# The first tile of x in four quarters over two DMA queues, in an attention and LoRA mixture layer

## The chip, the cores and the metric

The kernel runs on one core of a Trainium2 chip. The metric is the device time of one execution in microseconds, the median of several. One further execution is profiled; its page and trace are what this document reads. A core has TensorE (PE: matrix products, with weight loads shown as PEld), VectorE (DVE), ScalarE (ACT), GpSimd (POOL) and SyncE (SP), each with its own instruction queue; they wait for each other on semaphores. SP issues the DMAs that move data between HBM and the on-chip memory SBUF. Products land in PSUM, whose banks have to be copied out by DVE or ACT before they are used again.

## The reference

2048 tokens (4 sequences of 512) of width 1024, all in float32. Normalisation is without weights: subtract the mean, divide by the root of variance plus 1e-5.

```
x = x + layernorm(attention(layernorm(x)))
x = x + layernorm(ffn(layernorm(x)))

attention: qkv = x @ w_qkv.T + b_qkv           # 32 query heads, 8 key/value heads of 32
           rotate q and k (rope); causal softmax(q k.T / sqrt(32)) v; @ w_o.T + b_o
ffn:       logits = x @ gate_w.T; softmax over the best 2 of 8 experts, 0 for the others
           x @ base_w.T + base_b + 2 * sum over experts of weight * (x @ A.T) @ B.T   # rank 16
```

## The kernel before, in words

**Tiling.** The tokens are cut into 16 tiles of 128, one token a partition. A tile goes through: normalising x (`xa`, its statistics in `stats`), transposing it (`pt_xn`, copied out to `T_xn`), keys and values (`acc_kv`, then `raw_k` rotated and transposed as `pt_k`), queries (`acc_q`, `raw_q` rotated, transposed as `pt_q`, copied out to `qT`), attention, output projection (`acc_o`), two normalisations, transposes `pt_h`, gate and LoRA (`acc_gl`, `pt_low`) and the base product (`acc_f`).

**Pairs and mixed weights.** Queries, output projection and base product are computed for pairs of tiles with seven block products instead of eight (function `seven`), on sums and differences of activations (`s_q`, `s_o`, `s_f`) and of weights. The mixed weights are made once: `mix` loads rows, combines them on DVE or POOL (`mix_q`, `mix_o`, `mix_f`) and stores them to HBM. This takes place during the first third of the run. Weights for the products stream in as pieces of 128x512 (`piece`, L489) through a ring of 13.

**Attention.** A group is some heads of one tile: four rows of heads at once. Group t_a is tile t from head block a. Scores go to `sc` (L1446); DVE adds the causal mask (L1515) and takes the maximum (L1525) in two halves; ACT takes exponentials and their sums (L1467); DVE the reciprocal (`rtot`, L1496); POOL scales (`pr`, L1481); TensorE transposes each of the four parts (`pt_p`, L1541: pt_p_t_a_0 to _3), ACT or DVE copies them out (`prT`), and TensorE multiplies by the values (`av`, L1564).

**What sets the order.** The kernel is not scheduled by the framework. A planner inside it (`class Order`) goes through the work with assumed durations when the program is built. Chains of operations are Python generators that yield an `Op` (work for one of DVE, ACT, POOL, SP, with a time for each engine that may take it), a `Task` to wait for, or a delay in microseconds. The loop `tensor` always picks the next step for TensorE among the lanes (scores, transposes, values, dense products) by what the plan says is ready at the planned time; `_next` picks for the other engines. The order in which the planner decides is the order of each engine's instruction queue in the finished program; on the chip, semaphores alone decide when each starts. Every planned time feeds into later decisions, all through the plan.

**The first tile.** `load_x` brings a tile's x in two halves of 128x512 on SP (L870) and `normed_x` follows: statistics for each half as it lands (`Norm.half`, L524), the aggregate (L533), adding 1e-5 (L537), the root and the shift on POOL (L541, L545), scaling of the two halves on DVE or ACT (`Norm.apply`), transposes (L593). In the plan a DMA takes its kilobytes over 370 per microsecond on SP and lands 2.8 us later (`LANDS`). For the first tile (`jobs[0]`) nothing stands before it; after `job.issued` the loads of the key and value weights (`wkv_sb`, eight of 256 KB) follow on SP, then pieces, biases and the rotation table. All later tiles share the one buffer `xa`.

`Norm.quarter` (L502), statistics over 256 columns, is in the kernel already; it is used for the very last tile of tokens. Issued DMAs take eight completion semaphores in turn, so a DMA waits until the eighth before it has landed.

Of the kernel before, what the change touches and what calls it, by code (L numbers as in the profile page):

```python
# [91 lines left out]
class Order:  # L92
# [10 lines left out]
    def start(self, chain, at=0.0):  # L103
        task = Task()
        self._go_on(chain, task, at)
        return task
# [159 lines left out]
def kernel(  # L266
# [14 lines left out]
    nc = tc.nc  # L281
# [4 lines left out]
    NH = D // 512  # L286
# [29 lines left out]
    order = Order(banks)  # L316
    start = order.start

    def dve(us, urgent, issue):
        return Op(urgent, dve=(us, issue))  # L320
# [7 lines left out]
    def sp(us, issue, urgent=0):  # L328
        return Op(urgent, sp=(us, issue))
# [9 lines left out]
    def combine(urgent, out, in0, in1, op, engines=("dve", "pool")):  # L339
# [17 lines left out]
        out=earlier,  # L357
        in_=earlier,
# [17 lines left out]
    LANDS = 2.8  # L376
# [118 lines left out]
    class Norm:  # L495
# [6 lines left out]
        def quarter(self, src, k):  # L502

            if self.stats is None:
                self.stats = small.tile(
                    [P, 2 * NH, 6], F32, tag="stats4", bufs=1, name=f"stats_{self.name}"
                )
            cols = slice(k * 256, (k + 1) * 256)
            yield dve(
                0.4,  # L510
                self.urgent,
                lambda: nc.vector.bn_stats(out=self.stats[:, k, :], in_=src()[:, cols]),
            )
# [68 lines left out]
    def transposes(dst, src, halves, name, slot):  # L582


        steps, ready = [], []
        for h in range(NH):
            ready.append(Task())

            def issue(h=h):
                pt = ps.tile([P, 4, P], F32, tag="ps", name=f"pt_{name}_{h}")  # L590
                for c in range(4):
                    at = (4 * h + c) * P
                    nc.tensor.transpose(pt[:, c, :], src()[:, at : at + P], ident)  # L593

                def end():
                    yield step.done
                    yield copy(512, lambda: dst()[:, 4 * h : 4 * h + 4, :], lambda: pt)
                    banks.give(order.at)
                    ready[h].finish(order.at)

                step = steps_of[h]
                start(end(), order.now)

            steps.append(Step(0.44, issue, [halves[h], slot], bank=True, turns=True))
        steps_of = list(steps)
        return steps, ready
# [238 lines left out]
    jobs = [Job(tok, f"{tok.t}", has_q=tok.t != first) for tok in tokens]  # L845
# [7 lines left out]
    def load_x(job):  # L853

        yield xa_slots.take()
        if job is not jobs[0]:
            yield has_wk

        rows = slice(job.tok.t * P, (job.tok.t + 1) * P)
        job.xn = xpool.tile([P, D], F32, tag="xa", bufs=1, name=f"xa_{job.name}")  # L860

        def lands(h):
            yield LANDS
            job.in_x[h].finish(order.at)

        for h in range(NH):
            cols = slice(h * 512, (h + 1) * 512)
            yield sp(
                P * 512 * 4 / 1024 / RATE,
                lambda: nc.sync.dma_start(out=job.xn[:, cols], in_=x[rows, cols]),  # L870
            )
            start(lands(h), order.at)
        job.issued.finish(order.at)
# [14 lines left out]
    def normed_x(job):  # L888

        norm = Norm(f"1_{job.name}", 3)  # L890
        halves = [Task() for _ in range(NH)]

        def normed():
            for h in range(NH):
                yield job.in_x[h]
                yield from norm.half(lambda: job.xn, h)
            yield from norm.scale()
            for h in range(NH):
                yield from norm.apply(lambda: job.xn, lambda: job.xn, h)
                halves[h].finish(order.at)  # L900

        start(normed())
        taken = Task()

        def take_slot():
            yield halves[0]
            yield xnT_slots.take()
            taken.finish(order.at)

        start(take_slot())  # L910
        turns, job.ready = transposes(job.xnT, lambda: job.xn, halves, f"xn_{job.name}", taken)

        def free_x():
            yield [s.done for s in turns]
            xa_slots.give(order.at)

        start(free_x())
        return turns
# [720 lines left out]
    for job in jobs:  # L1639
        start(load_x(job))  # L1640
# [169 lines left out]
```

## Time and profile before

| | us |
|---|---|
| median of 3 runs | 1167.19 (1167.12 to 1168.61) |
| the profiled execution | 1167.07 |
| its span, first to last instruction | 1165.3 |
| TensorE busy (matmul) | 1139.3, 98% of the span |
| DVE, POOL, ACT busy | 829.1, 601.5, 529.2 |
| granted TensorE clock | 0.999 |
| share of the chain that ended last on TensorE | 90% |

A line of the profile's order of time has the start in us, the duration in us, engine, source line, operation, tile written <- tiles read, shape and count (a count over one merges neighbours). In square brackets stands how long the engine was idle before and what released it. A source line can be a helper's. Buffer numbers are left out of the tile names. A matrix product of 128x512 in float32 shows as two matmul records.

The first transposes of the first tile start at 7.34 us; the last product ends near 1157.8.

### The profile page before, as it was taken

The numbers are of one execution on the slowest core, as the hardware profiler recorded it, in microseconds if no ns is written. First come the engines' busy times: TensorE is split into PE (matmuls) and PEld (weight loads), VectorE is DVE, ScalarE is ACT, GpSimd is POOL, SyncE is SP. The second block draws the span as 40 slices with busy tenths as digits, with TensorE's granted clock in tenths as the row PEclk, the third lists the DMA queues.
The fourth block names the chain that finished last, engine by engine and source line by source line (L and its number), as shares of the span: only waits on it lengthen the run. The fifth ranks groups of instructions, "written<-read, shape, count | busy, mean of one in ns | idle before, by whom it ended". The sixth has DMA issues, their size and how long they took to land.

```text
span 1165.3 us, 21509 instructions
## 1 busy us (share of the span) xinstructions
PE 1139.3 (98%) x7284; PEld 632.8 (54%) x7284; DVE 829.1 (71%) x1635; ACT 529.2 (45%) x1543; POOL 601.5 (52%) x847
## 2 busy tenths in 40 slices
PE   7999999999999999999999999999999999999997
PEld 3555555655556555565555555456555555555455
DVE  4787878887777757688767775768866787668453
ACT  0354555445545355555534355455644555444011
POOL 2686846743756435555545353544645564446221
PEclk9999999999999999999999999999999999999999
DMA  9879778453772637635477443683457744574893
GB/s 346 290 244 316 248 251 286 168 173 104 252 242 80 211 103 248 188 95 165 144 244 253 141 140 109 197 262 102 144 173 230 243 139 160 179 261 144 274 317 117
DMA packets 118317, 232.54 MB, mean 200 GB/s; under 512 B 13504, under 2 KB 14528, under 8 KB 118208
## 3 DMA queue, kind: packets, MB, share of 16 engines
q1 hardware_dynamic: 118208, 231.16, 60.7%
q8 instruction: 59, 0.97, 0.3%
q14 instruction: 50, 0.41, 0.1%
HBM read 210.14 MB, written 20.97 MB: 198 GB/s over the span
## 4 chain that ended last, share of the span: by engine, by line
PE 90%; DVE 5%; ACT 2%; POOL 1%; issue 1%; DMA 1%; POOLq 0%; ACTq 0%; SPq 0%; DVEq 0%
PE acc_f L618 19%; PE acc_o L618 16%; PE acc_q L618 15%; PE pt_p L1541 12%; PE acc_kv L618 9%; PE sc L1446 7%; PE av L1564 6%; PE acc_gl L618 2%; PE pt_q L1013 1%; DVE nmax L1525 1%; PE pt_xn L593 1%; PE pt_h L593 1%; ACT pr L1467 1%; DMA xa<-in_x_dram 1%; DVE sc L1515 1%
## 5 line engine op out<-in xcount | busy, mean ns | idle before, releaser
L1481 POOL TENSOR_SCALAR pr<-pr,rtot 128x256 f32<-128x256 f32 (+3 forms) x512 | 306.7, 616 | 284.6 <-DVE rtot L1496 216.7
L1467 ACT ACTIVATE pr<-sc,nmax 128x256 f32<-128x256 f32 (+3 forms) x512 | 264.9, 536 | 122.2 <-DVE nmax L1525 65.3
L1525 DVE TENSOR_REDUCE nmax<-sc 128x2 f32<-128x768 f32 (+3 forms) x176 | 198.2, 1126 | 36.6 <-ACT pr L1467 33.4
L1541 PEld LDWEIGHTS pt_p<-ident,pr 128*128 128x128 f32 x1280 | 144.2, 141 | 59.0 <-issue 47.7
L1541 PE MATMUL pt_p<-ident,pr 128*128 128x128 f32 x1280 | 173.5, 276 | 2.7 <-DVE raw_k L951 1.1
L335 ACT COPY prT<-pt_p 128x512 f32<-128x512 f32 (+1 forms) x267 | 137.0, 548 | 77.9 <-PE pt_p L1541 75.0
L1515 DVE TENSOR_TENSOR sc<-sc,cmask 128x256 f32<-128x256 f32 (+2 forms) x176 | 96.6, 549 | 46.0 <-PE sc L1446 39.3
L618 PE MATMUL acc_kv<-wkv_sb,T_xn 128*128 128x512 f32 x256 | 120.5, 601 | 0.4 <-DVE prT L336 0.4
L335 ACT COPY aT<-av 128x128 f32<-128x128 f32 (+2 forms) x81 | 24.9, 308 | 202.6 <-PE av L1564 202.5
L618 PE MATMUL acc_f<-piece,T_h 128*128 128x512 f32 (+1 forms) x264 | 108.7, 541 | 0.0
L1467 ACT ACTIVATION_READ_ACCUMULATOR pr<-sc,nmax 128x1 f32 x512 | 108.5, 212 | 0.0
L618 PE MATMUL acc_q<-piece,s_q 128*128 128x512 f32 x224 | 105.4, 597 | 1.3 <-ACT prT L335 0.7
L618 PE MATMUL acc_o<-piece,aT 128*128 128x512 f32 x232 | 106.3, 594 | 0.0
L618 PE MATMUL acc_f<-piece,s_f 128*128 128x512 f32 x224 | 103.9, 594 | 0.5 <-ACT prT L335 0.5
L618 PE MATMUL acc_q<-piece,T_xn 128*128 128x512 f32 x224 | 103.6, 594 | 0.0
L618 PE MATMUL acc_o<-piece,s_o 128*128 128x512 f32 x224 | 102.8, 593 | 0.0
L1446 PE MATMUL sc<-kT,qT 32*128 32x384 f32 (+3 forms) x1024 | 93.9, 464 | 0.1
L343 POOL TENSOR_TENSOR y<-y,w 128x512 f32<-128x512 f32 x61 | 79.7, 1323 | 27.5 <-DVE w L562 12.9
L1564 PEld LDWEIGHTS av<-prT,v 128*32 128x32 f32 x2560 | 64.8, 109 | 51.3 <-issue 35.7
L1564 PE MATMUL av<-prT,v 128*32 128x128 f32 x2560 | 88.7, 276 | 0.2 <-DVE prT L336 0.2
L541 POOL TENSOR_TENSOR rstd<-veps,neg_half 128x1 f32<-128x1 f32 x64 | 36.2, 567 | 95.8 <-DVE veps L537 95.7
L336 DVE COPY prT<-pt_p 128x512 f32<-128x512 f32 (+1 forms) x85 | 54.7, 644 | 36.1 <-PE pt_p L1541 35.1
(157 smaller groups left out, 1407.2 us busy)
## 6 DMA issues: line engine op xcount, KB each, us to landing
piece<-in_w_o_dram SPq DMA_DIRECT2D x116, 256.0 KB, 3.5
piece<-in_w_base_dram SPq DMA_DIRECT2D x116, 256.0 KB, 3.5
piece<-mixed_q SPq DMA_DIRECT2D x112, 256.0 KB, 3.3
piece<-mixed_o SPq DMA_DIRECT2D x112, 256.0 KB, 4.1
piece<-mixed_f SPq DMA_DIRECT2D x112, 256.0 KB, 3.3
piece<-in_w_qkv_dram SPq DMA_DIRECT2D x100, 256.0 KB, 3.6
xa<-in_x_dram SPq DMA_DIRECT2D x32, 256.0 KB, 4.1
y<-in_x_dram SPq DMA_DIRECT2D x16, 512.0 KB, 6.0
```

Source lines behind the costliest of these rows:

```text
L335: act=(0.15 + n * 0.00085, lambda: nc.scalar.copy(out(), in_())),
L336: dve=(0.15 + n * 0.00105, lambda: nc.vector.tensor_copy(out(), in_())),
L343: engine.tensor_tensor(out=out(), in0=in0(), in1=in1(), op=op)
L541: nc.gpsimd.tensor_tensor(out=self.rstd, in0=self.veps, in1=neg_half, op=ALU.pow)
L618: nc.tensor.matmul(acc[0][:, :n], lhsT=lhsT(c), rhs=w(c), start=(c == 0), stop=last)
L1446: nc.tensor.matmul(sc[:, r, c * n : (c + 1) * n], lhsT=tok.qT[g.kt][rows, (g.at + c) % GROUP, :], rhs=seq.kT[g.kt][rows, :n], start=True, ...
L1467: lambda: nc.scalar.activation(pr[:, c * n : (c + 1) * n], sc4[:, r, c, :], AF.Exp, bias=nmax[:, r, c : c + 1], accum_out=total[:, r, c : ...
L1481: lambda: nc.gpsimd.tensor_scalar(pr[:, c * n : (c + 1) * n], pr[:, c * n : (c + 1) * n], rtot[:, r, c : c + 1], 1.0, ALU.mult, ALU.mult,),
L1515: lambda: nc.vector.tensor_tensor(out=diag, in0=diag, in1=cmask.unsqueeze(1).unsqueeze(1).to_broadcast([P, q, g.n, P]), op=ALU.add,),
L1525: lambda: nc.vector.tensor_reduce(nmax[:, some, : g.n], sc4[:, some], AX.X, ALU.max, negate=True),
L1541: nc.tensor.transpose(pt[:, j, :], g.pr[r][:, j * P : (j + 1) * P], ident)
L1564: nc.tensor.matmul(av[r * HD : (r + 1) * HD, c, :], lhsT=g.seq.v[j][:, head * HD : (head + 1) * HD], rhs=g.prT[r][:, c * (i + 1) + j, :], ...
```

## The change

Only the first tile is loaded differently: in four quarters of 128x256, the first and third issued by SP, the second and fourth by ACT, whose queue issued no DMA before. Its statistics are taken per quarter, each when its quarter has landed. In the plan, an issue of a quarter takes 0.4 us on its engine. The later tiles are loaded as before. ACT's queue starts with these two DMAs; the load of its function table, which stood first, follows them.

```diff
@@ def load_x(job):
+        def quarter(k):
+            cols = slice(k * 256, (k + 1) * 256)
+            on = {"act": nc.scalar, "sp": nc.sync}
+            engine = ("sp", "act")[k % 2]
+            issue = lambda: on[engine].dma_start(out=job.xn[:, cols], in_=x[rows, cols])
+            yield Op(0, **{engine: (0.4, issue)})
+            yield LANDS
+            job.in_x[k].finish(order.at)
+
+        if job is jobs[0]:
+
+            job.in_x = [Task() for _ in range(2 * NH)]
+            for k in range(2 * NH):
+                start(quarter(k), order.at)
+            job.issued.finish(order.at)
+            return
         for h in range(NH):
@@ def normed():
-            for h in range(NH):
-                yield job.in_x[h]
-                yield from norm.half(lambda: job.xn, h)
+            if job is jobs[0]:
+                for k in range(2 * NH):
+                    yield job.in_x[k]
+                    yield from norm.quarter(lambda: job.xn, k)
+            else:
+                for h in range(NH):
+                    yield job.in_x[h]
+                    yield from norm.half(lambda: job.xn, h)
             yield from norm.scale()
```

`job.issued` is finished as soon as the quarters are handed to the planner, at the plan's time 0, where before it was finished after the second half's issue.

## The prediction

> **What bounds the kernel now.** I read the page's busy table first, then busy time by stretch, TensorE's waits, and the order of time at two places.
>
> ```profile
> span 1165.3 us, 21509 instructions
> PE 1139.3 (98%) x7284; PEld 632.8 (54%) x7284; DVE 829.1 (71%) x1635; ACT 529.2 (45%) x1543; POOL 601.5 (52%) x847
> ```
>
> TensorE (PE) bounds: it is idle for 26 us in all. The stretches, first column length, second PE busy, put 6.0 of these at 48 to 390 us and 7.3 before the first transpose:
>
> ```profile
> 0.00:48.00 48.00, 40.66 (x136) 19.71 (x137) 27.00 (x51) 9.79 (x37) 18.13 (x31) 1.00 0.95 335
> 48.00:390.00 342.00, 335.97 (x2320) 190.10 (x2319) 269.63 (x518) 173.50 (x530) 217.82 (x304) 1.00 0.64 214
> ```
>
> The share 0.95 in the first row is DMA: the opening is also close to what DMA delivers. The opening in order of time:
>
> ```profile
> 0.79 0.86 SPq L870 DMA_DIRECT2D xa<-in_x_dram  x2
> 1.70 3.78 SPq L392 DMA_DIRECT2D wkv_sb<-in_w_qkv_dram  x8
> 3.65 0.69 DVE L524 BATCH_NORM_STATS2 stats<-xa 128x6 f32<-128x512 f32 x1 [3.65 <-DMA xa<-in_x_dram]
> 4.50 0.69 DVE L524 BATCH_NORM_STATS2 stats<-xa 128x6 f32<-128x512 f32 x1 [0.15 <-DMA xa<-in_x_dram]
> 5.23 0.21 DVE L533 BATCH_NORM_AGGREGATE mv<-stats 128x2 f32<-128x12 f32 x1
> 7.34 1.97 PE L593 MATMUL pt_xn<-ident,xa 128*128 128x128 f32 x8 [7.34 <-DVE xa L562]
> ```
>
> x lands, DVE takes statistics, PE starts at 7.34. What waits in 7 to 390 us, longest first (total, times, longest):
>
> ```profile
> PE pt_q L1013 <- DVE rtot L1496: 1.8, 1, 1.8
> PE pt_xn L593 <- DVE prT L336: 1.1, 1, 1.1
> PE pt_p L1541 <- DVE prT L336: 0.7, 1, 0.7
> PE acc_q L618 <- ACT prT L335: 0.7, 1, 0.7
> PE pt_k L962 <- DVE raw_k L788: 0.5, 1, 0.5
> ```
>
> **The first tile.** The sum is against the profiled execution, 1167.07 us (span 1165.3), 0.12 under the median 1167.19. Two statistics of 0.69 become four; a 128x256 one takes 0.43 and an aggregate over 24 values 0.26, by rows of the last tokens, where the kernel already does this:
>
> ```profile
> 1146.64 0.43 DVE L512 BATCH_NORM_STATS2 stats<-w 128x6 f32<-128x256 f32 x1
> 1158.76 0.26 DVE L533 BATCH_NORM_AGGREGATE mv<-stats 128x2 f32<-128x24 f32 x1
> ```
>
> After the last landing that is 0.43 + 0.26 instead of 0.69 + 0.21: 0.21 less. No row shows an x quarter or a DMA from ACT. The last issue stays at about 1.2 (two per queue of some 0.43 each instead of two on SP). Bounds for its landing: the first half took 2.86 from issue, giving 4.07; the quickest wkv_sb load took 4.0, giving 5.2. The second half landed at 4.50; as the same 512 KB lie ahead I take 4.5, so PE starts 0.2 earlier (0.5 later to 0.6 earlier). Of this I count 0.1, since near 22.5 us PE already meets a piece just as it lands.
>
> SP's queue. A load takes the next of eight semaphores and waits for the load eight before it. x now takes four, so wkv_sb loads 5 to 8 wait for x quarters (before: 7 and 8 for halves). Load 5 went out near 3.4 and now at the latest near 4.5; with the median 4.8 to land that is 9.3, and acc_kv needs it only after four products that start at 9.24. Behind it in SP stand the pieces; each waits for the same predecessor as before. Cost 0; up to 1 us if the quarters land late. ACT's table load (1.28 us at 0.78) now stands behind its two DMAs and the waits for tile 1's first half, which landed at 15.86; the scale it precedes needs POOL at 22.4, so some 4 us cover it.
>
> The skill's page "DMA: Bandwidth & Descriptors", section "Issuing engines are not separate DMA queues", speaks against the second queue: only issue time is saved. The rows say the same here, as the last issue does not move. [...]
>
> **The order of everything else.** The planner charges the first tile other times, so it places later work differently. Compared instruction by instruction, the two programs have the same matmuls of each kind. PE's order is equal up to 48 us and again from acc_q_6_6 (389.6 us) to the end; the other engines' orders also rejoin near there. Between lie 342 us with the same PE work, so only waits can differ. Spacings in this trace: a dense 128x512 product 0.86, four transposes 0.44, scores and values 0.8 to 1.1 a group; passing from dense to transposes costs nothing extra, and the passages into and out of scores and values, at 0.09 each, are as many in both.
>
> I therefore compared, in both orders, the PE work that lies between a result and its consumer. One place stands out, group 2_0 (tokens 2, heads 0):
>
> ```
> before: sc_2_0 av_1_4 pt_xn_5 pt_p_1_6 av_1_6 pt_q_3_1 acc_kv_5 x2 pt_p_2_0_0 sc_2_1 pt_p_2_0_1
>         acc_kv_5 x2 pt_p_2_0_2 pt_p_2_0_3 acc_kv_5 x3 ...
> after:  sc_2_0 av_1_4 pt_xn_5 pt_p_1_6 av_1_6 pt_q_2_1 pt_p_2_0_0 pt_p_2_0_1 sc_2_1
>         pt_p_2_0_2 pt_p_2_0_3 acc_o_0_0 x3 ...
> ```
>
> Before, pt_p_2_0_0 has 6.9 us of PE work behind sc_2_0, and the wait in front of pt_q_3_1 on top; after, 5.2. Nowhere else in the trace does such a transposition start less than 8.0 after its scores. The rows:
>
> ```profile
> 130.78 1.27 PE L1564 MATMUL av<-prT,v 128*32 128x128 f32 x28 [0.18 <-DVE prT L336]
> 133.84 0.63 PE L1013 MATMUL pt_q<-ident,raw_q 128*128 128x128 f32 x4 [1.78 <-DVE rtot L1496]
> 134.30 1.88 PE L618 MATMUL acc_kv<-wkv_sb,T_xn 128*128 128x512 f32 x4
> 136.02 0.49 PE L1541 MATMUL pt_p<-ident,pr 128*128 128x128 f32 x3
> 133.94 2.90 POOL L1481 TENSOR_SCALAR pr<-pr,rtot 128x384 f32<-128x384 f32 x3 [0.80 <-DVE rtot L1496]
> 136.81 1.27 POOL L783 TENSOR_TENSOR raw_q<-raw_q,rope_sb 128x512 f32<-128x512 f32 x1
> 138.60 1.27 POOL L343 TENSOR_TENSOR s_o<-s_o,aT 128x512 f32<-128x512 f32 x1
> ```
>
> The wait of the 133.84 row (2.6 us from where av_1_6's work would end, 131.2) stays: pt_q_2_1 waits for its own addition (L788), which now stands behind the same maximum on DVE. All is 0.53 earlier, pt_q_2_1 having left its place before sc_2_0. Then: pt_q_2_1 from 133.3 to 133.75. POOL's first scaling, at 0.97 (2.90 for three), runs 133.4 to 134.4, the second to 135.35. pt_p_2_0_0 waits 0.8, pt_p_2_0_1 0.6; sc_2_1 ends at 136.75. POOL's order now has s2_o_0 (1.27) and the rotation of raw_q_3_1 (1.27) ahead of pr_2_0_2, which at 0.59 (the bare scaling) is done at 138.5: pt_p_2_0_2 waits 1.9 and pt_p_2_0_3 0.25. Sum 3.5 us of new waits. It is 2.7 with all scalings at 0.59, and 4.3 if pt_p_2_1_0, now 7.6 behind its scores, needs the 8.4 it had. Queued behind on PE is all dense work: acc_kv_5 stands after pt_q_3_1 now.
>
> Waits that go, as the work in between grows: pt_k_2 0.7; the four transpositions of group 6_0 at 380 us 0.85 (9.6 us after their scores becomes 11.35); acc_q_4_5 at 233 us 0.85 (its bank now comes later). Together -2.4. Waits that come: six transpositions in a row (pt_p_3_0, pt_xn_6, near 207 us), each needing one of four PSUM banks that DVE or ACT copies must free. The nearest row is the 1.3 that such a row costs at 353 us (pt_xn behind DVE prT); +1.3, bounds 0 and 2. The pile at 353 itself stays, with pt_h_2 added and its dense cushion moved ahead. Shorter distances for pt_q_5_1 (7.8, was 21) and pt_low_3 (5.6, was 9.4) lie near the shortest seen unharmed (7.2 and 5.2): +0.5, bounds 0 and 1.5.
>
> Sum: -0.1 + 3.5 - 2.4 + 1.3 + 0.5 = +2.8, 1169.9 us. The ends: -0.6 + 2.7 - 2.4 + 0 + 0 = -0.3, and 1.0 + 4.3 - 1.6 + 2.0 + 1.5 = +7.2 (with a third of the lapsed waits back).
>
> **Rivals.** (1) Level. POOL is the mechanism: if it has done s2_o_0 and the rotation by the end of sc_2_1, the 1.9 and 0.25 vanish. It decides if POOL is at pr_2_0_2 before 136.7; against it, the two 1.27 rows after 135.35. Total +0.65, 1167.7. (2) Faster: the earlier first tile reaches the end and the 3.5 do not come, only lapsed waits: -0.6 - 2.4 = -3.0, 1164.1. For it: 6.0 us of PE's idle time lies in the reshuffled stretch; against: 5.2 against 8.0. (3) The quarters do not land earlier and the order costs more: bank waits at both piles and late quarters, +5, 1172.1. For it: the 353 us row, and DVE busy for 270 of 342 us in that stretch. That the change leaves the rest alone is excluded by the orders.
>
> **How the numbers follow.** Measurement tells about 0.2%, 2.3 us. Forecast (+1.3 to +4) 0.5, rival 1 0.28, rival 2 0.1, rival 3 0.12. Of the forecast 0.08 lies below 2.3 us; with rival 1 and 0.02 of rival 2 that is 0.38 within, slower 0.54, faster 0.08. The range goes from rival 2's nearer edge, 1166.4, to 1172.8 beyond rival 3.
>
> **What would show it.** Right: first statistics near 3.3 and the transposes within 0.5 of 7.34; PE idle in 48 to 390 near 9; a wait of about 2 before a pt_p of 128x384 near 137 with POOL at raw_q just before; the same gaps as now after 390. Wrong: no wait there, a hole in the first 48 us (quarters or wkv_sb late), or the difference arising after 390, where the order is equal.

## The result and the profile after

| | before | after |
|---|---|---|
| median, us | 1167.26 (1167.12 to 1168.61, 5 runs) | 1172.78 (1172.02 to 1173.85, 5 runs) |
| profiled execution, us | 1167.07 | 1173.85 |
| its span | 1165.3 | 1171.8 |
| granted TensorE clock in it | 0.999 | 0.994 |

The changed kernel is slower: ratio 1.0042, 95% interval 1.0028 to 1.0056. The forecast was 1169.9 within 1166.4 to 1172.8. The profiled execution of after is the longest of its five, so differences between the two traces (6.5 us in the span) are about 1 us larger than between the medians (5.5).

From the page of the changed kernel: span, busy time and the clock over 40 slices.

```profile
span 1171.8 us, 21502 instructions
PE 1143.4 (98%) x7284; PEld 633.8 (54%) x7284; DVE 826.2 (71%) x1618; ACT 535.4 (46%) x1559; POOL 604.9 (52%) x850
PEclk9999899999999999999999999999999999999999
```

TensorE is "busy" 4.1 us longer with the same 7284 matmuls, and one slice of the clock, the fifth (117 to 146 us), shows 8 where before has 9. So not all of the loss is idle time: part of it is matmuls that ran slowly.

The opening of the changed kernel in order of time (start, duration, engine, line, operation):

```profile
0.78 0.89 ACTq L870 DMA_DIRECT2D xa<-in_x_dram  x2
1.70 3.99 SPq L392 DMA_DIRECT2D wkv_sb<-in_w_qkv_dram  x8
3.40 1.50 DVE L512 BATCH_NORM_STATS2 stats<-xa 128x6 f32<-128x256 f32 x4 [3.40 <-DMA xa<-in_x_dram]
4.93 0.26 DVE L533 BATCH_NORM_AGGREGATE mv<-stats 128x2 f32<-128x24 f32 x1
7.10 1.97 PE L593 MATMUL pt_xn<-ident,xa 128*128 128x128 f32 x8 [7.10 <-DVE xa L562]
```

In this execution TensorE starts 0.24 earlier than in the one shown of before (7.10 against 7.34), and the weight loads leave SP at the same 1.70. The gain is gone at the first scores, which start 0.31 later than before; a wait for a weight piece, 0.6 in front of the product at 22.89 us, lies in between. Both are within what one execution differs from the next: over the traces of the experiments with two halves, or with quarters on two queues, the transposes start between 7.10 and 7.59, and the first scores, where their place in the order is the same, between 32.6 and 33.6.

The stretches of the changed kernel (bounds, length, then busy time of PE, PEld, DVE, ACT, POOL, the clock, DMA share, GB/s), the last three of them around group 2_0:

```profile
48.00:390.00 342.00, 333.83 (x2300) 188.71 (x2299) 261.58 (x487) 175.69 (x537) 218.28 (x299) 0.99 0.63 210
133.50:136.90 3.40, 1.52 (x31) 1.04 (x22) 3.02 (x5) 1.93 (x8) 2.52 (x3) 1.00 0.39 157
136.90:147.20 10.30, 8.68 (x25) 4.46 (x26) 7.13 (x13) 4.42 (x13) 7.88 (x9) 0.50 0.65 215
147.20:150.00 2.80, 2.80 (x38) 1.38 (x37) 2.77 (x7) 0.27 (x1) 2.80 (x4) 1.00 0.68 225
```

For 10.3 us the clock was halved. The whole difference arises before 390 us: the part of TensorE's order that is common to both to the end (from acc_q_6_6) starts at 389.61 before and 396.21 after, and takes 768.18 and 768.15.

What TensorE waited for in 7 to 390 us (total, times, longest), the longest of them:

```profile
PE pt_q L1034 <- DVE rtot L1517: 1.8, 1, 1.8
PE pt_p L1562 <- DVE prT L336: 1.7, 2, 1.1
PE pt_p L1562 <- POOL pr L1502: 1.6, 2, 0.9
PE pt_k L983 <- DVE raw_k L788: 1.4, 1, 1.4
PE acc_q L618 <- DMA piece<-in_w_qkv_dram: 0.6, 1, 0.6
```

The first is the wait that before has too, now in front of pt_q_2_1. The waits for pr are new. The one for raw_k stands in front of pt_k_4 near 116 us; before waited 0.5 for raw_k elsewhere, in front of pt_k_2. The waits of pt_xn and acc_q behind prT are gone.

Since the ends of matmuls are modelled, I count a wait below as the distance between the starts of two stretches of TensorE work, less what that distance is where nothing is waited for; products that ran slowly count too. Summed over 50 us at a time, this excess before and after is 2.7 and 3.3 (0 to 50), 1.5 and 1.7, **2.2 and 10.6 (100 to 150)**, 0.6 and 0.6, 2.0 and 2.6, 2.1 and 1.7, 0.3 and 0.3, **3.1 and 0.4 (350 to 400)**. One place costs 8.4, another gives 2.7 back.

That place in the changed kernel, TensorE and GpSimd in order of time:

```profile
136.16 0.63 PE L1034 MATMUL pt_q<-ident,raw_q 128*128 128x128 f32 x4 [1.78 <-DVE rtot L1517]
137.50 1.89 PE L1562 MATMUL pt_p<-ident,pr 128*128 128x128 f32 x6 [0.71 <-POOL pr L1502]
139.32 1.66 PE L1467 MATMUL sc<-kT,qT 32*128 32x384 f32 x8
141.91 1.54 PE L1562 MATMUL pt_p<-ident,pr 128*128 128x128 f32 x6 [0.93 <-POOL pr L1502]
143.25 4.70 PE L618 MATMUL acc_o<-piece,aT 128*128 128x512 f32 x6
147.88 0.93 PE L1467 MATMUL sc<-kT,qT 32*128 32x384 f32 x8
...
138.41 1.26 POOL L343 TENSOR_TENSOR s_o<-s_o,aT 128x512 f32<-128x512 f32 x1
140.03 1.26 POOL L783 TENSOR_TENSOR raw_q<-raw_q,rope_sb 128x512 f32<-128x512 f32 x1 [0.36 <-DVE turn_q L772]
141.28 1.15 POOL L1502 TENSOR_SCALAR pr<-pr,rtot 128x384 f32<-128x384 f32 x2
```

GpSimd does the two steps of 1.26 and only then the scalings that pt_p_2_0_2 (in the 141.91 row) waits for. Counted by starts the four transpositions wait 0.90, 0.66, 1.73 and 0.37. Then the six matmul records of acc_o_0_0 take 4.70; at the usual spacing of 0.43 they would take 2.74. The scores take 1.66 at 139.32 and 0.93 at 147.88. These are the halved clock. It also lies in the last of these waits: single transpositions start 0.22 apart here and 0.11 apart in before, so most of the 0.37 is slowness.

### The profile page after: what moved, and what is told of

Read it like the earlier page. It is cut to its first block, busy times and chain, and to the rows that moved or that the text cites. A ratio compares the mean times of both kernels' runs of the same rounds, so it can differ in the third digit from the quotient of the medians.

```text
span 1171.8 us, 21502 instructions
## 1 busy us (share of the span) xinstructions
PE 1143.4 (98%) x7284; PEld 633.8 (54%) x7284; DVE 826.2 (71%) x1618; ACT 535.4 (46%) x1559; POOL 604.9 (52%) x850
## 4 chain that ended last, share of the span: by engine, by line
PE 87%; DVE 5%; POOL 3%; DMA 2%; issue 1%; ACT 1%; POOLq 0%; ACTq 0%; SPq 0%; DVEq 0%
PE acc_f L618 19%; PE acc_o L618 16%; PE acc_q L618 14%; PE pt_p L1562 12%; PE acc_kv L618 7%; PE sc L1467 7%; PE av L1585 6%; PE acc_gl L618 2%; POOL pr L1502 1%; DVE nmax L1546 1%; DMA piece<-in_w_qkv_dram 1%; PE pt_h L593 1%; PE pt_q L1034 1%; PE pt_xn L593 1%; ACT pr L1488 1%
```

## The experiments

Theory: the loss is the re-planned order between 48 and 390 us, not the transfers. Rival: the transfers (second queue, shared semaphores, later table load) cost it. All times are medians; the kernel before had 1167.7 beside these runs.

| run | what | us |
|---|---|---|
| e1_kept_order | change's transfers, order of before | 1167.72 |
| e2_order_alone | transfers of before, order of after | 1173.36 |
| e5_one_queue | four quarters on SP, planned so | 1168.18 |
| e3_filled | after, waits at 2_0 filled with work | 1171.55 |
| e4_pool_order | after, GpSimd's order at 2_0 changed | 1172.49 |
| e9_filled_pool | both of these | 1173.08 |
| e10_filled_k | e3, GpSimd's order at raw_k_4 changed | 1170.28 |
| e6_late_plan | before, first tile planned 1.1 later | 1166.56 |
| e7_early_plan | before, first tile planned 1.2 earlier | 1176.87 |
| e8_rate_plan | before, transfers planned at 380 GB/s | 1168.02 |

### The change apart from its order, and the order apart from the change

e1 leaves the plan of before as it is and issues two quarters where it planned a half.

```diff
 # load_x and normed_x of the kernel before
-            yield sp(
-                P * 512 * 4 / 1024 / RATE,
-                lambda: nc.sync.dma_start(out=job.xn[:, cols], in_=x[rows, cols]),
-            )
+            def issue(h=h, cols=cols):
+                if job is not jobs[0]:
+                    nc.sync.dma_start(out=job.xn[:, cols], in_=x[rows, cols])
+                    return
+                for k, engine in ((2 * h, nc.sync), (2 * h + 1, nc.scalar)):
+                    q = slice(k * 256, (k + 1) * 256)
+                    engine.dma_start(out=job.xn[:, q], in_=x[rows, q])
+
+            yield sp(P * 512 * 4 / 1024 / RATE, issue)
 # normed(): for jobs[0] norm.quarters in place of norm.half
+        def quarters(self, src, h):
...
+            def issue():
+                for k in (2 * h, 2 * h + 1):
+                    cols = slice(k * 256, (k + 1) * 256)
+                    nc.vector.bn_stats(out=self.stats[:, k, :], in_=src()[:, cols])
+
+            yield dve(0.69, self.urgent, issue)
```

> The change's four transfers and four statistics, but every other instruction stays where the kernel before has it on all five engines. Theory (the loss comes from the re-planned order between 48 and 390 us): 1166.9 to 1167.9, the same as before; the first transpose some 0.2 earlier, and that gone again by 25 us in waits for weight pieces. Rival (the transfers cost: second queue, semaphores shared with the weight loads, table load later): 1171 or more, with the loss in the first 48 us.

e2 leaves the plan of after as it is and issues a half for every second quarter. "Order" here takes in which engine gets a step that two engines can do: the page of after counts 1618 instructions on DVE and 1559 on ACT, the page of before 1635 and 1543.

```diff
 # quarter(k) of the changed kernel
-            cols = slice(k * 256, (k + 1) * 256)
+            cols = slice(k * 256, (k + 2) * 256)
...
-            issue = lambda: on[engine].dma_start(out=job.xn[:, cols], in_=x[rows, cols])
+            def issue():
+                if k % 2 == 0:
+                    nc.sync.dma_start(out=job.xn[:, cols], in_=x[rows, cols])

 # normed(): norm.paired in place of norm.quarter
+        def paired(self, src, k):
...
+            cols = slice((k - 1) * 256, (k + 1) * 256)
+
+            def issue():
+                if k % 2:
+                    nc.vector.bn_stats(out=self.stats[:, k // 2, :], in_=src()[:, cols])
+
+            yield dve(0.4, self.urgent, issue)
```

> The order of the changed kernel on all five engines, but the first tile's x as before: two halves on one queue, two statistics. Theory: 1172.0 to 1174.0 like the changed kernel, with the same waits in front of the transpositions of group 2_0. Rival (the transfers cost): within 1 us of before, 1166.5 to 1168.3.

Measured: e1 1167.72, ratio to before 0.9999 (0.9990 to 1.0008, 11 runs); e2 1173.36, ratio 1.0044 (1.0031 to 1.0056). The stretch 48 to 390 us of e1, then of e2:

```profile
48.00:390.00 342.00, 335.94 (x2321) 190.03 (x2320) 271.07 (x518) 173.42 (x530) 217.85 (x303) 1.00 0.65 213
```

```profile
48.00:390.00 342.00, 333.69 (x2304) 188.93 (x2303) 262.76 (x489) 175.90 (x538) 218.52 (x300) 0.99 0.64 211
```

The first is like the row of before (335.97, clock 1.00), the second like that of after (333.83, clock 0.99). The order alone makes the loss, and the transfers alone make neither loss nor gain beyond the 1.2 us or so that the interval of e1 leaves open.

On average not even the first tile gains. The opening of e1:

```profile
3.58 0.75 DVE L524 BATCH_NORM_STATS2 stats<-xa 128x6 f32<-128x256 f32 x2 [3.58 <-DMA xa<-in_x_dram]
4.64 0.75 DVE L524 BATCH_NORM_STATS2 stats<-xa 128x6 f32<-128x256 f32 x2 [0.31 <-DMA xa<-in_x_dram]
5.43 0.26 DVE L546 BATCH_NORM_AGGREGATE mv<-stats 128x2 f32<-128x24 f32 x1
```

The third and fourth statistics run back to back: the fourth quarter (4.79) lands 0.17 after the third (4.62), while the statistic of the third is running. From there to the end of the aggregate it is 1.05 us (4.64 to 5.69), against 0.94 with a half (4.50 to 5.44). The last quarter also lands 0.16 later on average than a second half: at 4.45 to 4.79 in the six profiled executions with quarters on two queues, against 4.36 to 4.48 in the five with halves. The profiled execution of after is the exception: its third quarter was there at 4.11, so one statistic and the aggregate were left when the fourth landed at 4.45, and the aggregate ended at 5.20, as forecast. The six executions with quarters on two queues start the transposes at 7.10, 7.27, 7.31, 7.35, 7.42 and 7.59 (mean 7.34), the five with halves at 7.22, 7.22, 7.29, 7.31 and 7.34 (mean 7.28).

### The second queue and the plan

Why does the order flip at all? In the plan of after SP is done with x at 0.80 instead of 1.58, because ACT issues half of it and the rest is priced 0.4; and the first tile's aggregate is planned at 5.30 instead of 5.17, because four steps of 0.4 with a signal each last longer than two of 0.69. Relative to the weight loads the first tile is thus 0.91 later. The built programs bear this out: the kernel before with nothing changed but `LANDS + 0.9` for the first tile has the instructions of e2 in the same order on all five engines, while offsets tried from -0.8 to +0.7 leave TensorE's order of before as it was. On the chip SP gains none of the 0.78: the first weight load leaves at 1.70 in both. e5 keeps the quarters and takes the second queue away:

```diff
-            engine = ("sp", "act")[k % 2]
+            engine = "sp"
```

> Four quarters and four statistics, but all four transfers on SP and planned there. The planner then arrives at the order of the kernel before on every engine (only the first tile's own instructions differ). Theory (the loss is the order, and the second queue matters only because the planner counts SP free 0.8 us earlier): 1166.9 to 1168.5, the same as before; the four issues of some 0.43 each on one queue put the weight loads 0.9 later on SP, which costs at most 0.5. Rival (quarters or more transfers cost by themselves): 1170 or more.

Measured: 1168.18, ratio 1.0005 (0.9997 to 1.0014). The weight loads of e5 do go out 0.93 later, and the median is 0.5 above before, no more than the noise. A small cost is not excluded (the interval ends at 1.6 us): in its trace TensorE waits 1.2 by starts for a weight piece near 23.8 us, and the first scores start at 34.1. From its order of time:

```profile
2.63 3.75 SPq L392 DMA_DIRECT2D wkv_sb<-in_w_qkv_dram  x8
```

### The clock

e3 is the changed kernel with 50 needless transpositions of the identity into PSUM tiles that are about to be written anyway.

```diff
 # turn_q(k, h)
+            if (tok.t, h) == (2, 1):
+                for _ in range(20):
+                    nc.tensor.transpose(pt[:, 0, :], ident, ident)
 # turn(g, r)
+        if g.name == "2_0":
+            for _ in range((7, 5, 15, 3)[r]):
+                nc.tensor.transpose(pt[:, 3, :], ident, ident)
```

> The changed kernel with 50 needless transpositions (5.5 us of TensorE work at 0.109 each) put into the five waits at group 2_0, so that TensorE is busy while it waits. Theory (the three acc_o products behind the waits ran at 0.85 a matmul because the clock had dropped in the waits): the clock stays at 1.00 there, those products at 0.43, and the time 1.2 to 2.2 below the changed kernel, 1170.5 to 1171.6, although work was added. Rival (those products are slow by themselves, through their weight pieces or PSUM): they stay at 0.85 and the time is 1172.8 or more.

Measured: 1171.55 (1171.19 to 1172.80, 6 runs), 1.2 below after and 1.8 below e2; its slowest runs overlap with the fastest of after (1172.02). A stretch of e3:

```profile
138.00:142.00 4.00, 3.81 (x35) 2.86 (x33) 3.07 (x7) 1.15 (x3) 3.64 (x5) 1.00 0.53 178
```

and its TensorE in order of time:

```profile
138.26 0.93 PE L1470 MATMUL sc<-kT,qT 32*128 32x384 f32 x8
...
142.20 2.74 PE L618 MATMUL acc_o<-piece,aT 128*128 128x512 f32 x6
145.17 0.93 PE L1470 MATMUL sc<-kT,qT 32*128 32x384 f32 x8 [0.22 <-ACT pr L1491]
```

With TensorE kept busy the clock stays at 1.00 and acc_o_0_0 takes 2.74 instead of 4.70. The mean clock is 0.998 or 0.999 in all six executions, as it is with the kernel before; in five of after and five of e2 it lies between 0.993 and 0.997. More work made the kernel faster: the slow products were the clock's doing, and the clock's drop that of the waits.

### GpSimd's order at group 2_0

e4 holds two of GpSimd's instructions back until pr_2_0_3 has been scaled; every other engine keeps its order.

```diff
 # parts() of seven: s2_o_0, and rotate(): raw_q_3_1's product, are appended to `held` when planned
 # quadrant(r)
             g.normed[r].finish(order.at)
+            if (g.name, r) == ("2_0", 3):
+                for issue in held:
+                    issue()
+                held.clear()
```

> The changed kernel with one change of GpSimd's order: the scalings of pr_2_0_2 and pr_2_0_3 go ahead of s2_o_0 and of raw_q_3_1's product. Theory (GpSimd's queue makes pt_p_2_0_2 wait, 1.7): that wait shrinks below 0.4, the time is 1.0 to 2.0 below the changed kernel, 1170.8 to 1171.8; the clock still drops, since its cause lies earlier. Rival (something else, the exponentials or the sums, would hold it just as long): the wait stays above 1.2 and the time within 0.5 of the changed kernel.

Measured: 1172.49 (1172.00 to 1174.53), 0.3 below after. Theory and rival both fail in part. The wait went, the time did not. GpSimd and TensorE of e4 in order of time:

```profile
137.94 1.16 POOL L1506 TENSOR_SCALAR pr<-pr,rtot 128x384 f32<-128x384 f32 x2 [0.45 <-DVE rtot L1525]
...
139.97 1.54 PE L1570 MATMUL pt_p<-ident,pr 128*128 128x128 f32 x6
...
146.02 0.93 PE L1471 MATMUL sc<-kT,qT 32*128 32x384 f32 x8 [0.71 <-ACT pr L1492]
```

The transpositions at 139.97 wait for nothing, but the next scores, sc_2_2, now wait for the exponentials of group 2_1, which read the PSUM banks that sc_2_2 overwrites. The new theory: this wait stands right behind the one that GpSimd makes. e9 tests it with e3's filling and without its 18 transpositions in front of pt_p_2_0_2 and pt_p_2_0_3.

> The filled kernel (needless transpositions, clock held) with GpSimd's order mended as in the run on GpSimd's order, and without the 18 needless transpositions in front of pt_p_2_0_2 and pt_p_2_0_3. Theory (a next wait stands right behind the mended one: sc_2_2 can't be written before the exponentials of group 2_1 have read the same banks, 6.9 us after sc_2_1 in the filled run, which already waited 0.2 there): the 1.7 saved at pt_p_2_0_2 come back as a wait of 1.2 to 1.9 in front of sc_2_2, and the time is that of the filled kernel, 1171.1 to 1172.0. Rival (GpSimd was the bound, and only the clock hid its gain): 1169.8 to 1170.8.

TensorE of e9 in order of time, then a stretch of it:

```profile
138.80 0.93 PE L1474 MATMUL sc<-kT,qT 32*128 32x384 f32 x8
...
145.71 1.66 PE L1474 MATMUL sc<-kT,qT 32*128 32x384 f32 x8 [2.53 <-ACT pr L1495]
```

```profile
144.00:148.00 4.00, 2.29 (x24) 1.17 (x28) 3.82 (x9) 1.66 (x7) 3.55 (x4) 0.68 0.96 316
```

The time that GpSimd gave up stands in front of sc_2_2, which starts 6.91 us after sc_2_1 (138.80 to 145.71), as in e3 (138.26 to 145.17). So the place is set by the exponentials of 2_1, and GpSimd's order is worth nothing there as long as that wait stands. The median is 1173.08, above the 1171.1 to 1172.0 expected: in the profiled execution the new wait, 2.5 where 1.2 to 1.9 were expected, brings down the clock that the filling had held until then (0.68 in the last row, the scores at 1.66). In the five executions the mean clock lies between 0.996 and 0.999 and the time does not follow it one to one, so this explains the extra 1.5 only in part; the rest stays open.

### A wait that the prediction missed

The changed kernel's GpSimd near 116 us:

```profile
112.26 4.13 POOL L1502 TENSOR_SCALAR pr<-pr,rtot 128x256 f32<-128x256 f32 x6 [0.90 <-DVE rtot L1517]
116.36 0.72 POOL L783 TENSOR_TENSOR raw_k<-raw_k,rope_sb 128x256 f32<-128x256 f32 x1
```

Six scalings stand ahead of raw_k_4's product. In the kernel before it was four:

```profile
110.63 2.81 POOL L1481 TENSOR_SCALAR pr<-pr,rtot 128x256 f32<-128x256 f32 x4 [0.98 <-DVE rtot L1496]
113.40 0.72 POOL L783 TENSOR_TENSOR raw_k<-raw_k,rope_sb 128x256 f32<-128x256 f32 x1
```

e10 is e3 with the order of before at this place.

```diff
 # quadrant(r): the first scalings of pr_1_4_2 and pr_1_4_3 are held until raw_k_4's product is issued
+                late = g.name == "1_4" and r >= 2 and c == 0
+                issue = partial(behind_k.append, by_rtot) if late else by_rtot
```

> The filled kernel with one other change of GpSimd's order: the product of raw_k_4 goes ahead of the first scalings of pr_1_4_2 and pr_1_4_3, as in the kernel before. Theory (these two scalings make pt_k_4 wait 1.4 near 116 us in the changed kernel): that wait falls below 0.4 and the time is 0.8 to 1.5 below the filled kernel, 1170.0 to 1170.8. Rival (the two scalings, 0.7 later now, are waited for in its place): the sum of the waits of pt_k_4 and of the transpositions of group 1_4 stays, time 1171.1 to 1172.0.

Measured: 1170.28 (11 runs), 1.27 below e3. The wait for raw_k, 1.4 in after and 1.3 in e3, is 0.2 in e10, and nothing takes its place. From the waits of e10:

```profile
PE pt_k L989 <- DVE raw_k L794: 0.2, 1, 0.2
```

Here GpSimd's order was the bound. With the filling and this order together the kernel is still 2.6 above before. That rest is read from the trace only (the waits at group 2_0 that the filling occupies without shortening them, pt_p_3_1_3 and others, in the table below); no run takes it away.

### Other orders

If a few tenths of a microsecond in a plan decide between two orders that lie 5.5 us apart, other small errors of the plan should give other times. Three kernels change one planned number of the kernel before; the work stays, its order changes, and with it which engine gets a step that two can do.

```diff
-            yield LANDS
+            yield LANDS + (1.1 if job is jobs[0] else 0.0)     # e6; -1.2 in e7
```
```diff
-    RATE = 370.0
+    RATE = 380.0     # e8
```

> The kernel before, with its transfers and statistics, but the planner is told that the first tile's x lands 1.1 us later than it assumes otherwise. That gives a third order: PE work between scores and first transposition 6.7 at group 2_0 and 8.3 at 2_1 (before 6.9 and 8.3; changed kernel 5.2 and 5.4). Theory (these distances decide, and what is short of some 8.5 us is waited for): holes at 2_0 like those of before, no drop of the clock, 1166 to 1169.5. Rival (any order but the one that before has costs several us): 1171 or more.

> As the one before, but the planner is told 1.2 us earlier. The distances become 10.1 at group 2_0, 4.4 at 2_1 and 3.8 at 2_2. Theory: no hole at 2_0, but waits of some 4 us each at 2_1 and 2_2 (8.5 less the distance) and the clock dropping there: 1171 to 1177. Rival (the distances say little; waits move about and level out): 1166 to 1169.

> The kernel before, but the planner counts 380 instead of 370 GB/s for every transfer. Distances 6.6 at group 2_0, 8.6 at 2_1, none other below 9.0, and the shortest from keys to their transposition 4.3, 5.3, 6.4 (before 4.1, 4.3, 6.4). Theory: waits like before, 1165 to 1169. Rival (as in the runs above): 1171 or more.

Measured: e6 1166.56, ratio 0.9988 (0.9979 to 0.9997); e7 1176.87, ratio 1.0079 (1.0066 to 1.0093); e8 1168.02, ratio 1.0005 (0.9996 to 1.0014). All three times are inside what the distances gave, but the places are not. The longest waits of e7 before 390 us:

```profile
PE pt_q L1013 <- DVE raw_q L788: 4.2, 3, 3.5
PE pt_p L1541 <- POOL pr L1481: 2.7, 5, 0.8
PE sc L1446 <- ACT pr L1467: 2.1, 1, 2.1
```

The expected 4 us at the transpositions of groups 2_1 and 2_2 are not there; they stand in front of pt_q_2_1 and of sc_2_3. In e6 no wait as long as 0.3 is left at group 2_0, where holes like those of before were expected. And e8, with distances like those of before, has a hole of 4.4 us by starts, where before had 2.6, and a halved clock behind it (a row of the order of time, and a stretch):

```profile
136.12 0.63 PE L1013 MATMUL pt_q<-ident,raw_q 128*128 128x128 f32 x4 [3.41 <-DVE raw_q L788]
```

```profile
136.00:140.00 4.00, 3.88 (x19) 2.41 (x20) 2.80 (x6) 1.56 (x3) 4.00 (x5) 0.65 0.53 186
```

By its trace it is level with before because other waits of before, such as the 1.31 at 353 us, do not occur in it. e6 is a little faster than both kernels (1.15 us below before), without any of the change.

## Why the prediction was right, and where it was not

**Direction and cause: right.** Slower, through the order; "the passages" and everything after 390 us unchanged (768.18 against 768.15); transfers at cost 0 (e1, e5). Its signs came: first statistics at 3.40, a wait before pt_p_2_0_2 with GpSimd at raw_q just before. The size was too small: +2.8 forecast, +5.5 measured. That is above the band of +1.3 to +4 that the forecast itself held likely, and 1172.78 lies only 0.02 under the upper end of the range: that it lies inside is luck. The nearest figure was the +5 of rival 3. Its first condition came, the quarters land no earlier; the bank waits at both piles that it added did not (+0.1 near 207 us, and the 1.31 near 353 us went). Term by term, in the two profiled executions, where 6.6 us were to be explained:

| step of the sum | forecast | measured |
|---|---|---|
| first tile | -0.1 | +0.3 at the first scores |
| new waits at group 2_0 | +3.5 | +4.4 (0.90, 0.66, 0.41, 1.73, 0.37, 0.31) |
| waits that go (pt_k_2, 6_0, acc_q_4_5) | -2.4 | -2.4 (0.69, 0.86, 0.86) |
| six transpositions near 207 us | +1.3 | +0.1 |
| pt_q_5_1, pt_low_3 | +0.5 | 0 |
| halved clock at acc_o_0_0 | none | +2.0 |
| other new waits: pt_k_4 1.44, pt_p_3_1_3 1.27, pt_q_0_1 0.72, pt_p_1_2_3 0.71, pt_q_1_1 0.57, three of about 0.3 | none | +5.7 |
| other waits gone: 353 us 1.31, 251 and 254 us 0.88 and 0.70 | "stays" | -2.9 |

The right column sums to 7.2; the remaining -0.6 is in small waits that are not listed. Some of these come and go between executions of one order: pt_q_1_1, none in the trace of before, waits 0.66 in that of e1. The forecast's own terms come to 2.4, near its 2.8, though only because errors in them cancel; the terms that it lacks come to 4.8.

**The first tile.** The step "0.43 + 0.26 instead of 0.69 + 0.21" holds only when the third quarter is early enough, as in the profiled execution of after (transposes at 7.10, 0.24 earlier). In the other five traces with quarters on two queues two statistics are due at the end, not one, and over all six the last quarter lands 0.16 later than a second half. The price of a single statistic was right. The rule cited from the Trainium skill's page "DMA: Bandwidth & Descriptors", section "Issuing engines are not separate DMA queues", is what the runs show: the second queue spared SP 0.93 us of issuing (weight loads from 1.70, in e5 from 2.63), and the medians show nothing of it.

**Group 2_0.** Place, cause and nearly the size were right. But rival 1, which rested on it, was wrong: taking GpSimd's two steps out of the way (e4, e9) does not bring 1167.7, since the exponentials of 2_1 hold sc_2_2 to the same time. A forecast must ask what is next behind each wait, for the rivals too.

**"One place stands out."** This step failed. The sum has no term for pt_k_4, although the TensorE work between its keys and its transposition falls from 6.5 to 4.8 us; a distance of 4.3 is harmless for two other tiles (pt_k_0, pt_k_11), so the distance alone would not have told. What mattered was how many scalings stand ahead of raw_k_4's product in GpSimd's order, six instead of four (e10: 1.27 us). The terms near 207 us, pt_q_5_1 and pt_low_3, argued from TensorE's order and distances, did not come.

**The clock.** It was not in the sum at all. The trace of before has a hole of 2.6 us at the same place at full clock, and I took the new waits behind it as additive. Together they brought the clock down, which added 1.2 to 1.8 us (e3). By the last section the hole of before came close to doing so itself.

## What to carry to other kernels

Where a planner or scheduler orders the work, a change must be judged by the order it produces, and first with the old order kept (e1) and with the new order alone (e2): here the change itself was worth 0.0 us (within about 1.2) and the re-drawn order 5.6, and one planned number moved the same kernel between 1166.6 and 1176.9. When two orders are compared, look for each waiting instruction at what stands before its producer on that producer's engine, not only at the distance on the engine that waits; and before a wait is counted as a gain, name the wait behind it. On TensorE several waits close together can cost more than their sum, here 1.2 to 1.8 us more.

## What the runs showed of the hardware that was not expected

- TensorE's clock halves in the middle of a busy kernel. In after it fell near 136.9 and came back near 147.2 us: 10.3 us at 0.50. In the 3.4 us before the fall TensorE had been busy for 1.52. The Trainium skill, "TensorE: Matmul & The Clock Gate", section "Part 1: The HAM clock gate", tells of a free-running window of 3.4 us that decides the clock, and of half rate after an idle window. The 10.3 us fit three such windows, and the falls in the other traces last 6.8 us (e2, e4) or 3.4 us (e7, e8, e9); but here the time before the fall was not idle, only 45% busy, so where the page and the row differ, the row decides.
- The share that decides can be narrowed down from the twelve traces, if each is divided into steps of 3.41 us from the times at which its own clock changes. (The first change is the rise, at 11.96 us in before and 10.65 in after: up to there the matmul records of acc_kv start 0.85 apart, behind it 0.43.) Between 15 and 1155 us, all six falls follow a step in which TensorE was busy for 1.07 to 1.60 us (31 to 47%), and no step at full clock with 1.62 us or more was followed by one. The hole of 2.6 us in before lies nearly whole in one step with 1.62 us (131.42 to 134.83): its clock only just stayed up. In e5, of the same order, the same hole is spread over two steps with 2.57 and 2.27. So where a hole lies in the steps counts beside its length. The ends of matmuls are modelled, so the boundary is not known to 0.02 us.
- Two transfers of 128x256 on two queues are not both there before a transfer of 128x512 on one would be: the third quarter landed at 4.11 to 4.62 us and the fourth at 4.45 to 4.79 (six traces), the second half at 4.36 to 4.48 (five).
- The eight weight loads can leave SP 0.93 us later (e5) with the median within 0.5 us of before (ratio 1.0005, 0.9997 to 1.0014), although the DMA engines are busy for 0.95 of the first 48 us in the row of before.
